# Row halves of TensorE for graph products and transposes, and Strassen's form for a dense product, in a four-layer graph network

## The chip, the cores and the metric

The kernel runs on one core of a Trainium2 chip. The metric is the device time of one execution in microseconds (us). TensorE (PE; its weight loads are listed as PEld), VectorE (DVE), ScalarE (ACT) and GpSimd (POOL) each work through their own queue in order; SyncE (SP) issues most transfers. All data is fp32.

## The reference

The input x is 128 graphs x 64 nodes x 256 features, and adj is one 64 x 64 weighted adjacency matrix that all graphs share. Each of four layers computes `x = layernorm(x + f(x))`:

```python
# layer 0: two dense products with batch norms after a graph product
A_hat = D^-1/2 (adj + I) D^-1/2
agg = einsum('nm,bmd->bnd', A_hat, x)
h   = relu(batchnorm(agg @ W1.T + b1))            # 256 -> 512
f   = batchnorm(h @ W2.T + b2)                    # 512 -> 256
# layer 1: graph product, attention over the neighbours (4 heads), an MLP
lam = eigvalsh(adj)[-1] + 1e-8
L_norm = 2 adj / lam - I
h  = relu(layernorm((L_norm x) @ Wc + bc)); x1 = h + x
o  = softmax(mask(q k^T / 8)) v @ Wo + bo         # q, k, v from x1
x2 = layernorm(x1 + o)
f  = layernorm(x2 + gelu(x2 @ W1 + b1) @ W2 + b2)
# layer 2: two graph convolutions, then LSTMs over windows of 1, 2, 3, 4 nodes
h = relu(adj (x @ Wg0 + bg0)); h = relu(adj (h @ Wg1 + bg1))
for p in 1..4: h[last node of each window of p] = lstm_p(window)
# layer 3: graph attention
Wh = x @ W; e = leaky_relu(s1_i + s2_j); f = softmax(mask(e)) Wh
```

`eigvalsh` reads the lower triangle. Means and variances of layer 0's batch norms run over all 8192 rows.

## The kernel before

**Blocks.** Rows are cut into 16 blocks of 8 graphs. A block is 512 rows, held as 4 tiles `t` of 128 rows: a tile has two graphs, graph `q` on partitions 64q to 64q+63 (`halves` names the two ranges). Node-major tiles (`tm`) have rows on the partitions; feature-major tiles (`fm`) have features there. A graph product multiplies by a 128 x 128 block-diagonal matrix with the 64 x 64 matrix in both halves: `AhT` for layer 0, `LnT` for layer 1, `bdAT` for layer 2. So half of what TensorE multiplies with there is zero. `aggregate` (line 322) does 8 such products for a block and turns node-major rows into feature-major ones on the way. `to_fm` (334) and `to_tm` (340) transpose a block with 8 TensorE transposes, and `block` has 8 more for the attention weights (764).

**Buffers.** `PS` is a stock of four PSUM tiles of 128 x 1024 fp32, each two banks wide. `mem` is a stock of SBUF tiles of the same size, eight at first. `e_ps`, a PSUM tile, is taken for the eigenvalue and given back when layer 0 ends, so layer 0's blocks work with three.

**The order** is made while the program is built. Each block is a generator that yields `step(engine, us)` before it issues that step's instructions; `flow` keeps a planned time for each engine, and lets the step go next that can start first, with stock counts, priorities of the `Stream`s and a margin. The `us` in a step is only the planner's cost. The instructions then stand in that order in each engine's queue, and semaphores keep the dependencies.

**Layer 0** (lines 387 to 601). `first_block` loads x, does the graph product with AhT, copies it (537), makes 512 features in two halves with `W1T` (346), adds b1 on ACT (549) and takes statistics on DVE (553). When all 16 are done, `bn_coeffs` makes the first batch norm's scale and shift. `second_block` applies them with relu on ACT (561), multiplies 512 features by `W2T` in 16 matmuls of 128 x 512 (566), adds b2 (575) and takes statistics (579). Then comes the second `bn_coeffs`. `eig` finds the largest eigenvalue by squaring a matrix `EIG_STEPS` = 26 times. Each round squares (468), takes the trace by a DVE product and sum and a TensorE product with ones (471 to 476), and scales the square by its reciprocal (479, 481). It is a task among the blocks, the second in the list.

**After it.** `end_block` ends layer 0 (scale and shift, transpose back, residual, layer norm). `block` is layer 1: graph product with LnT, product with Wc (358), layer norm, `to_fm`, q, k (346) and v (705), scores (730), softmax, transposes (764), attention times v (778), Wo, layer norm, `to_fm`, the MLP (346, 835), two layer norms. `gcn_block` does two graph products with bdAT and the LSTM of window 1; `unit` does longer windows, where `lstm` already uses Strassen's form (1024). `last_block` ends layer 2 and is layer 3 (two transposes, 1404, 1450, 1460). Blocks of different layers overlap, except around the batch norms of layer 0.

**Queues.** SP issues x blocks, weights and output. Layer 1's weights go into `WA` and `WB`, which layer 0 doesn't use; `wL` and the weights after it go into memory that layer 0 frees. In the program's SP queue a transfer waits for what it overwrites, and for the transfer eight before it.

Of the kernel before, what the change touches and what calls it, by code (L numbers as in the profile page):

```python
# [11 lines left out]
ALU = mybir.AluOpType  # L12
# [21 lines left out]
def kernel(ctx: ExitStack, tc: tile.TileContext, a: dict, out: bass.AP):  # L34
# [282 lines left out]

    def aggregate(ps, y, mT):

        for c in range(2):  # L320
            for t in range(NT):
                T.matmul(
                    ps[:, c, t * P : (t + 1) * P],
                    y[:, t, c * P : (c + 1) * P],
                    mT,
                    start=True,
                    stop=True,
                )

    def to_fm(ps, y):  # L330

        for c in range(2):
            for t in range(y.shape[1]):
                T.transpose(ps[:, c, t * P : (t + 1) * P], y[:, t, c * P : (c + 1) * P], ident)

    def to_tm(ps, yT):

        for t in range(ps.shape[1]):
            for c in range(2):
                T.transpose(ps[:, t, c * P : (c + 1) * P], yT[:, c, t * P : (t + 1) * P], ident)  # L340
# [46 lines left out]
    with c0:  # L387
# [9 lines left out]
        W2T = ctile([P, 4, D], "W2T", wp)  # L397

        def later_loads():
            for k in cols:  # L400
                if k != "b1":
                    yield step("Q", 1.0)
                    nc.sync.dma_start(cols[k], a[f"L0_gnn_{k}"])
            yield step("Q", 6.0)
            nc.sync.dma_start(W2T, by_chunk(a["L0_gnn_W2"]))
            yield step("V", 1.2)
            V.tensor_tensor(adj2, bdA[:, :N], bdA[:, N:], ALU.add)

            V.tensor_scalar(cap1, adj2, 0.0, BIG, ALU.is_gt, ALU.mult)
            V.tensor_scalar(cap1, cap1, -1.0e9, None, ALU.add)  # L410

            V.tensor_scalar(cap3, adj2, 0.0, 2.0, ALU.not_equal, ALU.mult)
            V.tensor_scalar(cap3, cap3, -1.0, BIG, ALU.add, ALU.mult)
# [31 lines left out]

        def eig():
# [18 lines left out]
            for _ in range(EIG_STEPS):  # L465
                yield step("T", 0.5)
                pm = pse(P)
                T.matmul(pm, M, M, start=True, stop=True)
                yield step("V", 0.6)
                t_ = etile("etmp")  # L470
                V.tensor_tensor(t_, pm, ident, ALU.mult)
                d_ = etile("ed", 2)
                V.reduce_sum(d_[:, 0:1], t_, axis=AX.X)
                yield step("T", 0.4)
                p_ = pse(2)
                T.matmul(p_[:, 0:1], ones, d_[:, 0:1], start=True, stop=True)
                yield step("V", 0.5)
                r_ = etile("er", 1)
                V.reciprocal(r_, p_[:, 0:1])
                M = etile("eM")  # L480
                V.tensor_scalar(M, pm, r_, None, ALU.mult)
# [17 lines left out]
            V.tensor_tensor(LnT, t_, ident, ALU.subtract)  # L499

# [22 lines left out]
        def first_block(i):  # L523
            if i >= len(early):
                yield step("Q", 6.0, sl=1)
                xs = mem.take()
                nc.sync.dma_start(tm(mem[xs]), x_blk[i])
            else:
                xs = early[i]
            yield step("T", 1.8, ps=1, sl=1)  # L530
            ps = PS.take()
            ag = mem.take()
            aggregate(fm(PS[ps]), tm(mem[xs]), AhT)
            mem.give(xs)
            yield step("V", 1.25, ps=-1)
            aggT = fm(mem[ag])
            V.tensor_copy(aggT, fm(PS[ps]))
            PS.give(ps)
            for hf in range(2):
                dst = fm(Xs[i]) if hf == 0 else H[i]  # L540
                yield step("T", 3.45, ps=1)
                ps = PS.take()
                mm_fm(fm(PS[ps]), W1T, aggT, 2, off=2 * hf)
                if hf:
                    mem.give(ag)
                yield step("S", 1.3, ps=-1, waits=hf == 1)
                for c in range(2):
                    f = 2 * hf + c
                    S.activation(dst[:, c, :], fm(PS[ps])[:, c, :], AF.Identity, bias=cols["b1"][:, f : f + 1])
                PS.give(ps)  # L550
                yield step("V", 1.25, waits=hf == 1)
                for c in range(2):
                    V.bn_stats(st1[:, 2 * hf + c, i, :], dst[:, c, :])
            mark("l0a", i)

        def second_block(i):
            sc1, sh1 = bn["bn1"]
            src = [(fm(Xs[i]) if f < 2 else H[i])[:, f % 2, :] for f in range(4)]
            yield step("S", 2.8)
            for f in range(4):  # L560
                S.activation(src[f], src[f], AF.Relu, scale=sc1[:, f : f + 1], bias=sh1[:, f : f + 1])
            yield step("T", 6.9, ps=1)
            ps = PS.take()
            for c in range(2):
                for f in range(4):
                    T.matmul(
                        fm(PS[ps])[:, c, :],
                        W2T[:, f, c * P : (c + 1) * P],
                        src[f],
                        start=(f == 0),  # L570
                        stop=(f == 3),
                    )
            yield step("S", 1.3, ps=-1)
            for c in range(2):
                S.activation(H[i][:, c, :], fm(PS[ps])[:, c, :], AF.Identity, bias=cols["b2"][:, c : c + 1])
            PS.give(ps)
            yield step("V", 1.25)
# [6 lines left out]
        tasks[1:1] = [(None, eig, 0)]  # L584
        tasks[4:4] = [(None, later_loads, 0)]
# [7 lines left out]
        tasks += [(lambda: ready(("bn1",)), lambda i=i: second_block(i), 0) for i in blocks]  # L593
# [7 lines left out]
        flow([Stream(6, 0, tasks)], {"T": 2.0})  # L601
        PS.give(0)
# [5 lines left out]
        for k, w in zip(("Wc", "Wq", "Wk", "Wv", "Wo", "W1", "W2"), (Wc, Wq, Wk, Wv, Wo, W1, W2)):  # L608
            nc.sync.dma_start(w, by_chunk(a[f"L1_gnn_{k}"]))
# [21 lines left out]
    def end_block(i):  # L631
# [9 lines left out]
        yield step("T", 0.9, ps=1)  # L641
        ps = PS.take()
        to_tm(tm(PS[ps]), H[i])
        mark("h", i)
        yield step("V", 1.25, ps=-1)
        V.tensor_tensor(x, tm(PS[ps]), tm(mem[xin]), ALU.add)
# [5 lines left out]
    def block(i):  # L652
        x = X[i]
        mark("begun", i)
        yield step("T", 1.8, ps=1, sl=1)
        ps = PS.take()
        s_xp = mem.take()
        aggregate(fm(PS[ps]), x, LnT)
        yield step("S", 1.05, ps=-1)
        S.copy(mem[s_xp], PS[ps])  # L660
# [14 lines left out]
        yield step("T", 0.9, ps=1, sl=1)  # L675
        ps = PS.take()
        s_x1 = mem.take()
        to_fm(fm(PS[ps]), y)
        yield step("S", 1.05, ps=-1)
        x1T = fm(mem[s_x1])  # L680
        S.copy(mem[s_x1], PS[ps])  # L681
# [44 lines left out]
        for b in range(8):  # L726
            t, s = b // 2, b % 2
            for u in range(2):
                for r in range(2):
                    T.matmul(  # L730
                        pq[s * N : (s + 1) * N, r, 2 * t + u, :],
                        qT[r * N : (r + 1) * N, u, b * N : (b + 1) * N],
                        kT[r * N : (r + 1) * N, u, b * N : (b + 1) * N],
                        start=True,
                        stop=True,
                    )
# [22 lines left out]
        yield step("T", 0.9, ps=1, sl=1)  # L759
        ps = PS.take()  # L760
        s_a = mem.take()
        pt = PS[ps].rearrange("p (g m) -> p g m", g=8)
        for g in range(8):
            T.transpose(pt[:, g, :], e[:, g, :, :].rearrange("p r m -> p (r m)"), ident)
# [3 lines left out]
        S.copy(mem[s_a], PS[ps])  # L768
        PS.give(ps)
        yield step("T", 2.0, ps=1, sl=1)  # L770
# [3 lines left out]
        for b in range(8):  # L774
            t, s = b // 2, b % 2
            for u in range(2):
                for r in range(2):
                    T.matmul(
                        po[r * N : (r + 1) * N, u, b * N : (b + 1) * N],
                        v[r * N : (r + 1) * N, b, u, :],  # L780
                        aT[r * N : (r + 1) * N, 2 * t + u, s * N : (s + 1) * N],
# [18 lines left out]
        yield step("T", 0.9, ps=1, sl=1)  # L800
        ps = PS.take()
        s_x2 = mem.take()
        to_fm(fm(PS[ps]), y)
        yield step("S", 1.4, ps=-1)
        x2T = fm(mem[s_x2])
        for c in range(2):
            S.activation(
                x2T[:, c, :], fm(PS[ps])[:, c, :], AF.Identity, scale=g2c[:, c : c + 1], bias=be2c[:, c : c + 1]
# [394 lines left out]
    def gcn_block(i):  # L1203
        yield step("T", 1.8, ps=1, sl=1)
        ps = PS.take()
        s_a = mem.take()
        aggregate(fm(PS[ps]), X[i], bdAT)
# [5 lines left out]
        S.copy(mem[s_a], PS[ps])  # L1213
# [12 lines left out]
        yield step("T", 1.8, ps=1, sl=1)  # L1226
        ps = PS.take()
        s_a = mem.take()
        aggregate(fm(PS[ps]), h1, bdAT)
        mem.give(s_h1)  # L1230
        yield step("S", 1.05, ps=-1)
        S.copy(mem[s_a], PS[ps])
# [120 lines left out]
    def last_block(i, t0=0, nt=NT):  # L1353
# [14 lines left out]
        yield step("T", 0.9 * r, ps=1)  # L1368
        ps = PS.take()
        px = tm(PS[ps])[:, :nt, :]  # L1370
        to_tm(px, hb)
# [3 lines left out]
        V.tensor_tensor(x, px, x, ALU.add)  # L1375
# [3 lines left out]
        yield step("T", 0.9 * r, ps=1, sl=1)  # L1379
        ps = PS.take()  # L1380
        s_xT = mem.take()
        px = fm(PS[ps])[:, :, : nt * P]
        to_fm(px, x)


        yield step("S", 0.3 + 1.1 * r, ps=-1)
        xT = fm(mem[s_xT])[:, :, : nt * P]
        pairs, into = (ap.rearrange("p c (u e k) -> p c u e k", e=2, k=P) for ap in (px, xT))
        S.copy(into[:, :, :, 0], pairs[:, :, :, 0])
        for h in range(2):  # L1390
            S.copy(into[:, :, :, 1, halves[1 - h]], pairs[:, :, :, 1, halves[h]])
# [244 lines left out]
```

## Time and profile before

| | |
|---|---|
| three runs | 2438.67, 2440.18, 2441.17 us; median 2440.18 |
| the profiled execution | 2439.17 us; span from first to last instruction 2437.4 us |
| mean granted TensorE clock | 0.983 |
| first product stage of layer 0 | 8 to 155 us, PE busy throughout |
| second product stage | 161 to 276.5 us, PE busy throughout |
| waits of PE for its longest single release | 6.7 us, at the start (line 440) |
| granted clock in 283 to 427 us, where layer 1 begins | 0.93 |

The profile's page gives each engine's busy time and share of the span. A row such as `L322 PE MATMUL ps<-LnT,x 128*128 128x128 f32 x16` is line, engine, operation, output and inputs (moving operand first), the rows and columns of the array in use, the moving size, and the count. One fp32 matmul of the program is two loads and two matmul records; an fp32 transpose is one of each. In a timeline the first two numbers are the start and the length in us, and equal records that follow each other are one row. In a table of stretches each engine's busy time is followed by its record count, then come granted clock, DMA share and GB/s.

### The profile page before, as it was taken

Reading aid. Unit: us, or ns where it says so; the run is one execution under the profiler, and the core shown is the slowest. Engines: PE = TensorE matmul, PEld = TensorE weight load, DVE = VectorE, ACT = ScalarE, POOL = GpSimd, SP = SyncE. Lnnn points to the kernel's source line nnn. Section 1 sums busy time; section 2 is a strip of 40 time slices with the busy share of each in tenths; the row PEclk is TensorE's granted clock in tenths of the full one; section 3 lists DMA queues with packets and bytes.
Section 4 is the critical chain, followed back from the end, with each engine's and each line's share of the span. In section 5 each row is a group of like instructions: output and inputs, shape, how many; then the busy total and the mean of one; then the engine's idle time right before and its main releaser. Section 6 shows DMA issues by size and latency. Waiting matters only on the chain. (4 is left out here: it accounts for less than half of the span.)

```text
span 2437.4 us, 33965 instructions
## 1 busy us (share of the span) xinstructions
PE 2348.3 (96%) x13700; PEld 1798.9 (74%) x13700; DVE 1215.1 (50%) x2864; ACT 1169.9 (48%) x2138; POOL 566.7 (23%) x426
## 2 busy tenths in 40 slices
PE   8999889999999999999999999999999999998997
PEld 5544567766676666676676788899999888887785
DVE  4542377646475345744462433344435444455446
ACT  2255453543444444335544444444444654468766
POOL 0000034222333222422231221222212222122112
PEclk9999989999999999999999999999999999999998
DMA  5110111000000000000010000000001000001111
GB/s 172 44 52 0 40 31 49 27 9 10 1 10 18 10 9 10 1 10 34 20 61 1 18 1 1 1 18 1 1 1 35 1 9 10 18 27 66 40 35 44
DMA packets 40974, 57.47 MB, mean 24 GB/s; under 512 B 4592, under 2 KB 33904, under 8 KB 40816
## 3 DMA queue, kind: packets, MB, share of 16 engines
q1 hardware_dynamic: 39712, 54.22, 6.9%
q8 instruction: 107, 1.75, 0.3%
q10 hardware_dynamic: 1104, 1.08, 0.1%
q14 instruction: 51, 0.42, 0.1%
HBM read 38.52 MB, written 16.78 MB: 23 GB/s over the span
## 5 line engine op out<-in xcount | busy, mean ns | idle before, releaser
L1024 PE MATMUL ps<-x,x 128*128 128x256 f32 x1024 | 248.6, 380 | 0.7 <-DVE t L1092 0.7
L1024 PEld LDWEIGHTS ps<-x,x 128*128 128x128 f32 x1024 | 191.5, 190 | 26.4 <-issue 1.6
L314 ACT ACTIVATE x<-x,ln_nm,ln_rs 128x256 f32<-128x256 f32 x196 | 103.7, 592 | 97.0 <-DVE ln_nm L311 95.5
L1024 PE MATMUL ps<-t,x 128*128 128x256 f32 x576 | 141.0, 379 | 0.0
L308 POOL TENSOR_TENSOR ln_rs<-ln_rs,neghalf 128x4 f32<-128x4 f32 (+1 forms) x72 | 70.5, 980 | 231.1 <-DVE ln_rs L274 217.3
L1024 PEld LDWEIGHTS ps<-t,x 128*128 128x128 f32 x576 | 108.6, 190 | 14.6 <-issue 0.4
L346 PE MATMUL ps<-t,W1T 128*128 128x512 f32 x256 | 115.2, 593 | 0.0
L952 PE MATMUL ps<-h,wL 128*128 128x192 f32 (+2 forms) x504 | 111.6, 375 | 0.0
L952 PEld LDWEIGHTS ps<-h,wL 128*128 128x128 f32 x504 | 79.1, 190 | 27.6 <-issue 26.7
L272 DVE BATCH_NORM_STATS2 ln_st<-x 128x6 f32<-128x256 f32 x256 | 98.2, 404 | 0.5
L1100 ACT ACTIVATE t<-t,bih 128x512 f32<-128x512 f32 (+2 forms) x63 | 41.0, 652 | 107.6 <-DVE t L1090 105.9
L952 PE MATMUL ps<-h,x 128*128 128x256 f32 x384 | 86.8, 379 | 0.0
L964 ACT ACTIVATE t<-ps,bih 128x512 f32<-128x512 f32 (+3 forms) x104 | 61.5, 642 | 44.0 <-PE ps L952 43.9
L294 POOL TENSOR_TENSOR ln_rs<-ln_rs,neghalf 128x4 f32<-128x4 f32 x32 | 36.9, 1153 | 188.8 <-DVE ln_rs L274 188.6
L346 PEld LDWEIGHTS ps<-t,W1T 128*128 128x128 f32 x256 | 46.3, 190 | 46.4 <-issue 46.4
L952 PEld LDWEIGHTS ps<-h,x 128*128 128x128 f32 x384 | 72.9, 190 | 10.3 <-issue 0.5
L1083 DVE COPY t<-ps 128x256 f32<-128x256 f32 (+2 forms) x63 | 23.7, 378 | 113.5 <-PE ps L1024 113.5
L273 DVE BATCH_NORM_AGGREGATE ln_mv<-ln_st 128x2 f32<-128x6 f32 x448 | 71.3, 167 | 0.0
L346 PE MATMUL ps<-t,wA 128*128 128x512 f32 x144 | 67.9, 617 | 2.8 <-ACT t L681 2.8
L952 PE MATMUL ps<-t,wL 128*128 128x512 f32 x144 | 64.9, 607 | 2.5 <-ACT t L1250 2.5
L1090 DVE TENSOR_TENSOR t<-ps,t 128x512 f32<-128x512 f32 (+2 forms) x63 | 38.1, 604 | 54.8 <-PE ps L1024 47.9
L1100 ACT ACTIVATE x<-x,bih 128x512 f32<-128x512 f32 (+2 forms) x57 | 36.6, 641 | 55.7 <-DVE x L1090 55.4
(692 smaller groups left out, 5688.2 us busy)
## 6 DMA issues: line engine op xcount, KB each, us to landing
t<-in_x_dram SPq DMA_DIRECT2D x26, 512.0 KB, 3.9
xd<-x SPq DMA_DIRECT2D x16, 512.0 KB, 2.6
x<-xd SPq DMA_DIRECT2D x6, 512.0 KB, 3.3
out_dram<-x SPq DMA_DIRECT2D x6, 512.0 KB, 3.0
wL<-in_L_gnn_Wih_dram SPq DMA_DIRECT2D x2, 1024.0 KB, 4.9
h<-in_x_dram SPq DMA_DIRECT2D x4, 512.0 KB, 4.2
x<-in_L_gnn_Whh_dram SPq DMA_DIRECT2D x2, 1024.0 KB, 4.9
t<-xd SPq DMA_DIRECT2D x4, 512.0 KB, 3.3
```

What stands on the lines that cost most here:

```text
L272: V.bn_stats(st[:, t, :], y[:, t, :])
L273: V.bn_aggr(mv[:, t, :], st[:, t, :])
L294: G.tensor_tensor(rs, rs, neghalf[:, :NT], ALU.pow)
L308: G.tensor_tensor(rs, rs, neghalf[:, :n], ALU.pow)
L314: S.activation(y[:, t, :], y[:, t, :], AF.Identity, scale=rs[:, t : t + 1], bias=nm[:, t : t + 1])
L346: T.matmul(ps[:, c, :], w[:, k, (off + c) * P : (off + c + 1) * P], yT[:, k, :], start=(k == 0), stop=(k == nk - 1),)
L952: T.matmul(spread(fm(PS[ps])[:, j, :n], q), WL[p][0][:, k, m], x_of(0, q)[:, k], start=(k == 0), stop=(k == 1),)
L964: S.activation(of(sl)[:, j], fm(PS[ps])[:, j, :n], AF.Tanh if g == 2 else AF.Sigmoid, bias=bias(g, c))
L1024: T.matmul(dst, WS[p][name](k, g), y[:, k], start=first and k == 0, stop=k == 1, skip_group_check=not first)
L1083: V.tensor_copy(y[:, 1, :], v[:, 0, :])
L1090: V.tensor_tensor(y[:, 0:2, :], v[:, 2:4, :], y[:, 0:2, :], ALU.add)
L1100: S.activation(of(act[g])[:, 0], of(act[g])[:, 0], f, bias=bias(g, 0))
```

## The change

1. `aggregate`, `to_fm`, `to_tm` and the attention transposes issue each 128-row product as two of 64 rows, one on each half of the array's rows, with the 64 x 64 diagonal block or half of the identity as the moving operand. The two halves' outputs go to different banks of the PSUM tile (`part`), and the copies out of PSUM put them together again (`joined`, `runs`).
2. Attention times v sends the output of row half r to column half r ^ u. The columns of Wq, Wk and Wv are loaded in another order to match, in three transfers each. The scores' loops are reordered, and `last_block`'s copies follow its transposes.
3. `second_block` does blocks 1 to 15 in Strassen's form: seven products of 256 x 256 by 256 x 256 in place of eight, in two-matmul pairs, with four sums of the weights made once (`W2S`, in `WB[:, 2:4]`) and the input and output sums on DVE, POOL and ACT. Block 0 keeps eight products, one feature chunk behind each relu.
4. `eig` is in a stream of its own with first priority; only each third round scales by the trace, and it gives its PSUM tile back when it ends.
5. The planner's costs are lower: 0.95 for 1.8 (graph product), 0.5 for 0.9 (transposes), 1.3 for 2.0 (attention times v).

```diff
+    def part(ps, s, g):
+        return ps[:, s * TB + g * N : s * TB + (g + 1) * N]
+    def joined(ps, n=2 * NT):
+        return ps.rearrange("p (s g e) -> p g s e", s=2, e=N)[:, :n]
...
     def aggregate(ps, y, mT):
         for c in range(2):
             for t in range(NT):
-                T.matmul(
-                    ps[:, c, t * P : (t + 1) * P],
-                    y[:, t, c * P : (c + 1) * P],
-                    mT,
+                for s, h in enumerate(halves):
+                    T.matmul(
+                        part(ps, s, c * NT + t),
+                        y[h, t, c * P : (c + 1) * P],
+                        mT[h, h],
...
-                T.transpose(ps[:, c, t * P : (t + 1) * P], y[:, t, c * P : (c + 1) * P], ident)
+                for s, h in enumerate(halves):
+                    T.transpose(part(ps, s, c * n + t), y[h, t, c * P : (c + 1) * P], ident[h, h])
...
+            V.tensor_tensor(W2S[0], a21, a22, ALU.add)
+            V.tensor_tensor(W2S[1], W2S[0], a11, ALU.subtract)
+            V.tensor_tensor(W2S[2], a11, a21, ALU.subtract)
+            V.tensor_tensor(W2S[3], a12, W2S[1], ALU.subtract)
...
-            for _ in range(EIG_STEPS):
+            for j in range(EIG_STEPS):
...
+                if j % 3 < 2:
+                    yield step("V", 0.35)
+                    M = etile("eM")
+                    V.tensor_copy(M, pm)
+                    continue
...
-            V.tensor_copy(aggT, fm(PS[ps]))
+            V.tensor_copy(runs(mem[ag]), joined(PS[ps]))
...
+            V.tensor_tensor(T1, x[:, :, v], x[:, :, u], ALU.subtract)
+            V.tensor_tensor(T2, h[:, :, v], T1, ALU.subtract)
+            G.tensor_tensor(T4, h[:, :, u], T2, ALU.subtract)
+            V.tensor_tensor(T3, h[:, :, v], x[:, :, v], ALU.subtract)
...
+            product(A11, x[:, :, u], p[:, 0, :], first=True)
+            product(W2S[0], T1, p[:, 3, :], first=True)
+            S.copy(y[:, 0, :], p[:, 0, :])
+            S.copy(y[:, 3, :], p[:, 3, :])
+            product(A12, h[:, :, u], p[:, 2, :])
+            product(W2S[3], h[:, :, v], p[:, 3, :])
+            product(W2S[1], T2, p[:, 0, :])
+            V.tensor_copy(y[:, 1, :], p[:, 0, :])
+            product(W2S[2], T3, p[:, 0, :])
+            V.tensor_tensor(y[:, 3, :], p[:, 0, :], y[:, 3, :], ALU.add)
+            V.tensor_tensor(y[:, 0:2, :], p[:, 2:4, :], y[:, 0:2, :], ALU.add)
+            product(A22, T4, p[:, 0, :])
...
-        flow([Stream(6, 0, tasks)], {"T": 2.0})
-        PS.give(0)
+        flow([Stream(1, 0, [(None, eig, 0)], urgent=True), Stream(6, 1, tasks)], {"T": 2.0})
...
+            if k in ("Wq", "Wk", "Wv"):
+                for m, j in ((slice(0, P), slice(0, P)), (slice(P, P + N), slice(P + N, 2 * P)), (slice(P + N, 2 * P), slice(P, P + N))):
+                    nc.sync.dma_start(w[:, :, m], src[:, :, j])
...
-                        po[r * N : (r + 1) * N, u, b * N : (b + 1) * N],
-                        v[r * N : (r + 1) * N, b, u, :],
-                        aT[r * N : (r + 1) * N, 2 * t + u, s * N : (s + 1) * N],
+                        po[halves[r ^ u], u, b * N : (b + 1) * N],
+                        v[halves[r], b, u, :],
+                        aT[halves[r], 2 * t + u, s * N : (s + 1) * N],
```

## The prediction

> **What bounds the kernel now.** I read the page's busy shares first, then the stretches of the span, then TensorE's own timeline at a fine scale.
>
> ```profile
> span 2437.4 us, 33965 instructions
> PE 2348.3 (96%) x13700; PEld 1798.9 (74%) x13700; DVE 1215.1 (50%) x2864; ACT 1169.9 (48%) x2138; POOL 566.7 (23%) x426
> ```
>
> TensorE is busy for 96% of the span and every other engine for half or less. The same by stretch (span, then busy time of PE, PEld, DVE, ACT, POOL):
>
> ```profile
> 161.00:276.50 115.50, 115.50 (x291) 53.28 (x290) 28.27 (x64) 62.81 (x94) 0.00 (x0) 0.98 0.00 0
> 283.00:427.00 144.00, 127.86 (x1005) 95.74 (x1005) 101.93 (x281) 77.70 (x113) 54.07 (x38) 0.93 0.17 51
> 427.00:1160.00 733.00, 713.25 (x4905) 497.35 (x4904) 402.49 (x902) 317.44 (x403) 217.95 (x132) 0.98 0.04 12
> 1160.00:2135.00 975.00, 971.14 (x5170) 839.67 (x5169) 431.89 (x856) 446.04 (x939) 227.06 (x163) 1.00 0.04 12
> 2135.00:2437.40 302.40, 269.36 (x1749) 224.23 (x1747) 162.56 (x570) 220.58 (x522) 63.43 (x77) 0.96 0.13 43
> ```
>
> PE's idle time is 16 us at the start of layer 1, 20 us in the rest of layers 1 and 2, 33 us at the end. Everywhere else the time is TensorE's stream, so an edit is priced by what it does to that stream. PE's busy time alone can't price it (the tail of each matmul overlaps the next); I use the distance from one row's start to the next row's start:
>
> ```profile
> 424.50 1.84 PE L905 MATMUL ps<-av,t 128*128 128x1 f32 x16
> 661.12 1.21 PE L730 MATMUL ps<-t,h 64*64 64x64 f32 x64
> 662.26 2.05 PE L322 MATMUL ps<-LnT,x 128*128 128x128 f32 x16
> 664.25 2.08 PE L778 MATMUL ps<-x,t 64*64 64x64 f32 x64
> 2184.31 1.04 PE L334 MATMUL ps<-ident,h 128*128 128x128 f32 x8
> 2185.19 1.04 PE L334 MATMUL ps<-ident,x 128*128 128x128 f32 x8
> 1996.13 0.68 PE L1450 MATMUL ps<-ident,x 64*64 64x64 f32 x16
> 1996.74 0.70 PE L1024 MATMUL ps<-x,x 128*128 128x256 f32 x2
> 1997.28 0.59 PE L1024 MATMUL ps<-h,x 128*128 128x256 f32 x2
> ```
>
> Each fp32 matmul leaves two records; a transpose leaves one. "rows*columns" is the part of the array used. Read from it:
> - A transpose costs 0.88/8 = 0.11 us. A graph product costs 1.8 to 2.0 us for 8 matmuls, 0.112 us a record.
> - L905 streams one column, and still takes 1.84 us for 16 records, 0.11 us each after the last one's tail. So **loading 128 columns of weights takes 0.11 us by itself**; a graph product, which also streams 128 columns, is already limited by its loads.
> - L730 runs 64 records on 64x64 parts in 1.14 us, L778 the same number in 2.01 us. L730 keeps all four quarters at work: its loads of both row halves and both column halves overlap. L778 uses only the two quarters on the diagonal.
> - Changing the split costs time. Two records of 256 columns take 0.43 us. Around L1450: it takes 0.61 us where its 16 records at L778's pace (2.01/64) take 0.50, and the two L1024 records after it take 0.54. With 0.1 us before its start, going in and out costs about 0.35 us, **0.17 us a change**.
>
> [...] a load record on 64 rows and 64 columns (L1450) has a median of 135 ns, on 128 rows and 64 columns (L705) 137 ns, on 128x128 (L322) 192 ns. No row here loads 64 rows by 128 columns. [...]
>
> **The change part by part.** Counts are from the two programs' instruction orders.
>
> (a) Graph products: 64 groups (16 with AhT, 16 with LnT, 32 with bdAT). 512 matmuls on 128x128 become 1024 on 64x128. Streaming halves, but each half still loads 128 columns. With both row halves loading side by side, a round of two half-records takes 0.112 us, and there are 16 rounds, as there were 16 records: 64 x 16 x (0.112 - 0.112) = **0**. Bounds: if a load of 64 rows took half, a round would take 0.058 us: -64 x 16 x 0.054 = -55 us. If the halves loaded one after the other, +64 x 16 x 0.112 = +115 us. I take 0, by L905 and the equal 64- and 128-row loads.
>
> (b) Transposes: 768 instructions, or 96 groups of 8 (16 groups where layer 0 ends, 48 in layer 1, 32 in the last blocks). A transpose's load is shorter (L334's load record: a median of 141 ns, near the 135 of a 64-column load), so its 0.109 us is streaming. That halves to about 0.058, the spacing of L1450's rounds [...]: -96 x 8 x 0.051 = **-39 us**. If its loads go one after the other: about +6.
>
> (c) Attention's product with v, 16 groups: outputs cross (r ^ u), so four quarters work: 2.01 -> about 1.05 us, **-15**. Nothing gained: 0.
>
> (d) Scores: same products reordered; L730 is at four quarters already: **0**, at most a tenth of 1.14 us either way, 2 us over 16 blocks.
>
> (e) Strassen's form, 15 of 16 blocks: before, 32 records of 512 columns, 16 matmuls, 6.87 us (four rows of 1.72). After, 14 matmuls of 256 columns, 28 x 0.2155 = 6.03 us. -15 x 0.84 = **-12.5**. What it adds elsewhere per block: DVE three differences at 0.68 (L1339), a copy at 0.42 (L1083) and sums at 0.69 + 0.41 (L1090, L1092), 3.6 us; ACT two copies at 0.37 (L1062) and one more eviction, 1.1 us; POOL one difference, 1.3 us (L983). In this stage ACT rises from 63 to about 80 us, DVE from 28 to about 72 (the eigenvalue's work leaves it), against some 100 of PE: covered, by the blocks in flight, which get four PSUM tiles in place of three. The last blocks have no cover for the chain product, sum, product: **+3**. If the hops aren't hidden, +20.
>
> (f) Eigenvalue: 18 of 26 ones-products go, about 0.25 us each: **-4.5**. The chain runs wholly inside the first product stage, where PE is always busy; between the stages (155 to 161, 277 to 283) statistics still hold PE, since the last copy, bn_stats, bn_aggr and coefficients remain. Bound: 4 us more if the urgent squarings make PE wait, as PE runs its queue in order and everything behind them waits too; 4 less if the stalls shrink.
>
> (g) Split changes: 151 in the order before, 340 after. 189 x 0.17 = **+32**. Bound: 0.1 to 0.2 each, +19 to +38.
>
> (h) Evictions through a view that alternates between two PSUM banks every 64 elements: same element count (ACT 1.01 us, DVE 1.22). L743 already writes in runs of 64 without a price (678 ns for 512, like L1242). Taken as 0; ACT and DVE have the slack; at most 5 us where they end a wait.
>
> (i) Transfers: Wq, Wk, Wv in three pieces each, six more SP issues of about 0.5 us at 12 to 25 us, where x blocks are queued between them; the fourth x block is needed only at about 35 us. The load of W2 into wB now waits for the last Strassen product, at the end of layer 0, with wL, the small weights and two x blocks behind it; wL waited until 283.56 before as well. Four x blocks are ahead of it, where six were. Taken as 0; +3 if those two are late. W2S's four DVE sums wait for W2T, issued at 10.76 and landed by 15.97, when Wo could use its semaphore; the DVE queue behind holds the first evictions: at most 2 us.
>
> Sum: 0 - 39 - 15 - 12.5 + 3 - 4.5 + 32 = **-36 us**, of which I drop 2 for the last 240 us, where PE isn't always the limit: -34. The profiled execution took 2439.17 us (span 2437.4 and 1.8 around it), 1.0 below the median 2440.18. 2439.2 - 34 = 2405 in its terms, **2406** against the median.
>
> **The rivals.**
> 1. Half loads are half as long. L905 and the pair of 135 and 137 ns speak against it, but no row has this shape. It adds -55: 2351. Together with small gains elsewhere, 2340.
> 2. The two row halves load one after the other when each is 128 columns wide. Then (a) is +115, (b) +6 in place of -39: -34 + 115 + 45 = +126, 2566. L730 speaks against it, where row halves do overlap, but with columns split as well. It decides from the round's length: with all else as summed, the change turns slower once a round in (a) takes 0.112 + 34/1024 = 0.145 us.
> 3. The PE time is saved but not kept: Strassen's hops (+20) and waits in layer 1's ramp and at the end (10), where PE idles already. 2406 + 30 = 2436, no change.
> 4. That the halves don't come about at all is excluded: the order shows 16 instructions of 128x64 for every 8 of 128x128.
>
> **How the numbers follow.** About 0.2% (5 us) is what a measurement of this kernel can tell from no change. Own forecast (2390 to 2430): 0.52. Rival 1 (2338 to 2365): 0.24. Between my forecast and rival 3, up to 2440: 0.11, of which 0.06 is within 0.2%. Rival 2: 0.08. Other losses (evictions that wait on banks, an order that fits badly): 0.05. Faster 0.81, same 0.06, slower 0.13. The range 2338 to 2440 leaves out rival 2 and the other losses; without rival 1 it would begin at 2390.
>
> **What would show it.** Right: PE rows of a graph product (16 matmuls, 32 records) still 1.8 us or more from start to start, and next to other splits 0.35 longer; 8 halved pairs of transposes about 0.5 us; attention's product about 1 us; the second product stage about 100 us in place of 115.5; no ones-product after the first barrier. Wrong: a graph product in about 1 us (rival 1) or 3.6 (rival 2), PE idle inside the second stage above 5 us (rival 3), or ACT copies above 1.1 us.

## The result: no change

The changed kernel took 2440.78 us, the median of 12 runs (2436.29 to 2446.48), against 2440.2 before: a ratio of 1.0007, 95% interval 0.9998 to 1.0016. The forecast was 2406, with a range up to 2440.0. None of the 34 us appeared. The profiled execution took 2446.48 us, the slowest of the twelve, 5.7 above the median, and the profiled execution of the kernel before is 1.0 below that kernel's median; so of any difference between the two profiles about 7 us belong to the executions and not to the kernels.

The page of the changed kernel, its span and its busy times:

```profile
span 2444.7 us, 38027 instructions
PE 2323.0 (95%) x15636; PEld 1789.4 (73%) x15636; DVE 1255.6 (51%) x2904; ACT 1185.4 (48%) x2168; POOL 591.0 (24%) x441
```

TensorE is busy 25 us less than before, and the span is 7 us longer: what it saved, it waits. Most of those 7 us belong to the two profiled executions, as said above. The stretches of the changed kernel (span, busy time of PE, PEld, DVE, ACT, POOL, then granted clock, DMA share, GB/s), cut at its own stages:

```profile
8.00:166.40 158.40, 157.86 (x842) 93.19 (x840) 77.73 (x149) 40.49 (x63) 0.56 (x1) 1.00 0.25 70
172.20:276.20 104.00, 101.25 (x436) 82.35 (x436) 69.89 (x121) 76.48 (x140) 21.59 (x15) 0.98 0.08 25
280.70:427.00 146.30, 122.63 (x1198) 87.48 (x1199) 105.58 (x275) 77.84 (x114) 52.96 (x33) 0.86 0.17 53
427.00:1160.00 733.00, 707.59 (x5871) 477.61 (x5870) 413.70 (x920) 316.78 (x406) 225.57 (x136) 0.99 0.04 15
2135.00:2444.70 309.70, 267.32 (x1925) 220.48 (x1924) 157.01 (x554) 214.46 (x496) 62.68 (x76) 0.95 0.12 38
```

The first product stage ends at 166.4 us, 11 later than before (155). The second takes 104.0 where it took 115.5. The start of layer 1 has 24 us of idle TensorE where it had 16, and a clock of 0.86 where it had 0.93. From 427 to 1160 the idle time is 25 us, before 20.

Each operation of layers 0 and 1 nevertheless costs what the prediction said. TensorE's timeline of the changed kernel:

```profile
352.57 1.95 PE L340 MATMUL ps<-LnT,x 64*128 64x64 f32 x32
354.45 1.16 PE L884 MATMUL ps<-h 64*64 64x64 f32 x64
...
434.16 2.00 PE L340 MATMUL ps<-bdAT,x 64*128 64x64 f32 x32
436.00 0.67 PE L870 MATMUL ps<-ident,t 64*128 64x64 f32 x16
436.50 0.67 PE L361 MATMUL ps<-ident,h 64*128 64x64 f32 x16
```

From start to start, a halved graph product takes 1.84 us (434.16 to 436.00), what the full one took. Eight halved transposes take 0.50 (436.00 to 436.50; 0.88 before). Attention's product is a row of 1.16 where it was 2.08.

**Where the time went.** I gave every TensorE record the distance to the next start that it has when nothing disturbs it (429 ns for 512 columns, 216 for 256, 112 for a record of a full graph product, 56 for a halved one, 109 and 29 for a full and a halved transpose). What exceeds it I put down to idle time (the record had ended before the next began), to a split change (rows or columns of the array differ in the next record), or to the rest (half clock, and the LSTM's own irregular spacing, taken as about the same in all). In this part of the span the granted clock was 0.50 for 64 us in the kernel before and for 83 in the changed one. How much of the LSTM counts as stream and how much as rest is a choice, so only the differences between the rows are read. From the first transposes of layer 0's end to TensorE's last start, in us:

| kernel | layer 0 ends | undisturbed stream | idle | split changes | rest | sum after layer 0 |
|---|---|---|---|---|---|---|
| before | 282.6 | 1872 | 78 | 18 | 178 | 2145 |
| changed | 280.8 | 1818 | 109 | 36 | 192 | 2155 |
| e2, planner's cost 1.8 | 283.4 | 1818 | 86 | 36 | 183 | 2122 |
| e1, full products too | 275.7 | 1818 | 87 | 31 | 180 | 2115 |
| c2, planner's cost 1.4 | 279.8 | 1818 | 115 | 36 | 203 | 2173 |
| f5, order of before | 285.0 | 1818 | 102 | 31 | 188 | 2139 |

The stream is 54 us shorter, as predicted (39 + 15). Idle time took 31 of it back, split changes 18, the rest 14: 63 in all, of which about 7 belong to the two profiled executions. By stretch, the idle time grew by 8 us at the start of layer 1 and by 9 at the end (the two tables of stretches), and by 8 between 427 and 1300 us.

### The profile page after: what moved, and what is told of

The parts are those of the page before. It is cut to its first block, busy times and chain, and to the rows that moved or that the text cites. A ratio compares the mean times of both kernels' runs of the same rounds, so it can differ in the third digit from the quotient of the medians.

```text
span 2444.7 us, 38027 instructions
## 1 busy us (share of the span) xinstructions
PE 2323.0 (95%) x15636; PEld 1789.4 (73%) x15636; DVE 1255.6 (51%) x2904; ACT 1185.4 (48%) x2168; POOL 591.0 (24%) x441
## 5 line engine op out<-in xcount | busy, mean ns | idle before, releaser
L1134 PE MATMUL ps<-x,x 128*128 128x256 f32 x864 | 212.9, 381 | 1.6 <-DVE x L1193 1.0
L1134 PEld LDWEIGHTS ps<-x,x 128*128 128x128 f32 x864 | 160.6, 190 | 25.2 <-issue 2.0
L1134 PE MATMUL ps<-t,x 128*128 128x256 f32 x704 | 170.0, 380 | 0.0
L1134 PEld LDWEIGHTS ps<-t,x 128*128 128x128 f32 x704 | 132.9, 190 | 18.9 <-issue 0.8
L1062 PE MATMUL ps<-h,wL 128*128 128x192 f32 (+2 forms) x456 | 90.4, 352 | 0.0
L272 DVE BATCH_NORM_STATS2 ln_st<-x 128x6 f32<-128x256 f32 x224 | 85.4, 403 | 0.4
L1062 PEld LDWEIGHTS ps<-h,wL 128*128 128x128 f32 x456 | 70.1, 190 | 16.8 <-issue 15.8
L1062 PE MATMUL ps<-t,wL 128*128 128x512 f32 x168 | 73.7, 594 | 1.3 <-ACT t L1360 0.7
L1074 ACT ACTIVATE x<-ps,bih 128x512 f32<-128x512 f32 (+3 forms) x84 | 48.9, 634 | 52.3 <-PE ps L1062 52.1
L1062 PE MATMUL ps<-x,wL 128*128 128x512 f32 x144 | 62.9, 593 | 0.0
```

Of the source, the lines that this page charges most:

```text
L272: V.bn_stats(st[:, t, :], y[:, t, :])
L1062: T.matmul(spread(fm(PS[ps])[:, j, :n], q), WL[p][0][:, k, m], x_of(0, q)[:, k], start=(k == 0), stop=(k == 1),)
L1074: S.activation(of(sl)[:, j], fm(PS[ps])[:, j, :n], AF.Tanh if g == 2 else AF.Sigmoid, bias=bias(g, c))
L1134: T.matmul(dst, WS[p][name](k, g), y[:, k], start=first and k == 0, stop=k == 1, skip_group_check=not first)
```

## The experiments

All times are medians; ratios are to the kernel before, with their 95% intervals. Theory C blames halved products (a late clock), theory I or W the waits for ACT and DVE, theories P, R and O the order in which the planner puts the steps (P: a planned cost below the true time makes a worse order; R: one near the true time makes a good order; O: each order is a draw, good or bad by chance).

**e1, e2, e3, e4: graph products put back in full, or the planner's cost alone.**

```diff
 e1: aggregate_full: one T.matmul(fm(ps)[:, c, t*P:(t+1)*P], y[:, t, c*P:(c+1)*P], mT), at all 4 places
+    V.tensor_copy(mem[ag], PS[ps]); S.copy(mem[s_xp], PS[ps]); S.copy(mem[s_a], PS[ps])
-    yield step("T", 0.95, ps=1, sl=1)
+    yield step("T", 1.8, ps=1, sl=1)
 e2: the last two lines alone        e3: as e1, in first_block alone
 e4: aggregate_full if i < 2, in first_block and block; costs as in the changed kernel
```

> The changed kernel with only its graph products put back: 64 groups of 8 products on 128 x 128, copied out of PSUM in plain order, planned at 1.8 us; transposes, attention and layer 0 stay changed. Theory C (halved products keep TensorE at half rate after every idle stretch, and add split changes): about 6 us back in the first stage, about 5 at the start of layer 1, and 59 fewer split changes at 0.13 us, 8: 2422 us. Theory I (the time that TensorE saves is lost to waits for ACT and DVE, whatever form the products have): no change, 2436 to 2445. Theory P (an order planned with a product at 0.95 us that takes 1.8 fits badly): faster by 10 to 20, but then the kernel with the planner's cost alone is as fast.

> The changed kernel with the planner's cost of a graph product put back from 0.95 to 1.8 us, nothing else: the same instructions in another order. Theory P (order planned with a wrong cost): faster by 10 to 20 us, with PE's idle time in layers 1 and 2 down by that. Theories C and I: no change beyond 5 us either way, clock at the starts as in the changed kernel.

> The changed kernel with graph products on 128 x 128 in layer 0 alone. Theory C: first product stage ends 8 to 9 us earlier (5.8 by a clock that comes up after 4 us of work as before, where the changed kernel's records stay at double spacing until 25.7 us; 20 split changes at 0.13, 2.6), total 2432 us; layer 1 as in the changed kernel, its clock 0.5 until about 300 us less 9. Theory I: the stage is shorter by the split changes at most, total 2438 to 2441.

> The changed kernel with full products in blocks 0 and 1 of layers 0 and 1 only (4 of 64 groups), the planner's costs and nearly all split changes (338 for 340) as there. Theory C, in its narrow form (only the start of a stretch matters; once at full rate the halves keep it): full rate before 15 us in place of 25.7, and about 4 us earlier in layer 1; total 2430 to 2433. Theory I, or if the rate is lost again in the halved groups that follow: no change, 2438 to 2443.

Measured: e1 2401.6 (0.984, 0.9827 to 0.9854), e2 2416.7 (0.9904, 0.989 to 0.9917), e3 2435.0 (0.9981, 0.9974 to 0.9987), e4 2437.6 (0.9991, 0.9984 to 0.9998). The surprise is e2: **one number in the planner, with the same instructions, is worth 24 us.** e1 is 15 below e2, and that is the halved products. e3's first stage ends 7.0 us earlier than the changed kernel's (158.9 for 165.9, by TensorE's last start in it), e4's 4.4. Theory C holds for the starts, but it is the smaller part: e3 is 6 us faster than the changed kernel (its planned cost of 1.8 in layer 0 changes the order too; e4's order stays), and e4, with 4 full groups of 64, only 3, where C's narrow form expected 8 to 11. Theory I as stated (the same loss in whatever form) falls.

Where the order puts a wait, the queue behind it stops too: between 378.5 and 384.2 us no PE record starts. From the changed kernel's timeline:

```profile
377.40 1.12 PE L367 MATMUL ps<-h,wA 128*128 128x512 f32 x2
384.26 5.16 PE L367 MATMUL ps<-h,wA 128*128 128x512 f32 x8 [5.74 <-DVE t L901]
...
389.26 3.60 PE L367 MATMUL ps<-h,wB 128*128 128x512 f32 x8
```

The next product waited 5.74 us for a sum on DVE. After it, eight records took 5.16 us where the next eight took 3.60: the granted clock was 0.50 from 385 to 387 us and 1.00 from 388 on, and 1.5 us more went with it. PE's waits between 300 and 1300 us (line, what it waited for, us in total, times, longest), first the changed kernel:

```profile
PE ps L367 <- ACT t L786: 9.1, 2, 5.6
PE ps L367 <- DVE t L901: 7.1, 2, 5.7
PE ps L354 <- DVE t L778: 5.0, 1, 5.0
```

and e2:

```profile
PE ps L354 <- ACT h L786: 6.2, 1, 6.2
PE ps L354 <- DVE t L778: 5.0, 1, 5.0
PE ps L367 <- ACT t L786: 2.3, 1, 2.3
```

The wait for L901 isn't among e2's, but e2 waits 6.2 us for L786 at the same place, and the eight records after it are as slow, 5.85 us:

```profile
382.48 1.12 PE L354 MATMUL ps<-ident,t 64*128 64x64 f32 x16 [6.16 <-ACT h L786]
383.53 5.85 PE L367 MATMUL ps<-h,wA 128*128 128x512 f32 x8
```

So these long waits are not the difference; they show what a wait costs. No single wait makes the 24 us. Idle time after layer 0 is 86 us in place of 109, and most of that lies between 427 and 1300 us, where layers 1 and 2 overlap and no wait is over 3.5 us: TensorE is idle there for 27 us in the changed kernel and for 9 in e2. The mean granted clock is 0.985 in e2 and 0.979 in the changed kernel (rest 183 for 192).

**c1, c2: the planner's cost, in the kernel before and at a middle value.**

```diff
 c1, kernel before:    -yield step("T", 1.8, ...)   +yield step("T", 0.95, ...)   (4 graph products)
 c2, changed kernel:   -yield step("T", 0.95, ...)  +yield step("T", 1.4, ...)
```

> The kernel before with one number changed: the planner's cost of a graph product 0.95 us in place of 1.8, while the product itself stays as it was. Theory P (a cost below the true time makes orders in which TensorE waits): slower by 10 to 24 us, 2450 to 2464, with the loss in PE's idle time of layers 1 and 2. Theory O (any other order would do it; the kernel with 1.8 was only lucky): anywhere within 15 us to either side.

> The changed kernel with the planner's cost of a graph product at 1.4 us, between its own 0.95 and the true 1.8. Theory P: between the two, 2422 to 2434. Theory O: no relation to the cost, as likely outside.

Measured: c1 2451.7 (1.0047, 1.0035 to 1.0059), as P expects, and as O allows. c2 2465.7 (1.0104, 1.0091 to 1.0117): not between 2441 and 2417 but 25 above the higher. P falls.

**c3, c4: one part alone on the kernel before.** c3 takes the new `aggregate` and its copies with the old cost; c4 the new transposes, their copies and their new costs.

> The kernel before with only its 64 graph products in row halves and the copies that follow, planned at 1.8 us as before. Theory C (rate and split changes): 110 more split changes at 0.13 us, 14; about 6 at the start and 5 at layer 1's start by the late clock: slower by 20 to 27, 2460 to 2467. Theory N (halves cost nothing but the split changes, the late start is something else): slower by 10 to 15, 2450 to 2455.

> The kernel before with only its 96 groups of transposes in row halves, their copies and their planned costs (0.5 for 0.9). Working of the prediction with the split change at the 0.13 us that the changed kernel's trace shows: 39 saved, 124 more split changes, 16: faster by 23, 2417. If waits for DVE and ACT take the place of what TensorE saves: 2430 to 2440. If halved transposes too keep the clock down at layer 1's start: 3 less saved than by the first.

Measured: c3 2465.3 (1.0105, 1.0092 to 1.0118), as C expects. Its order is that of the kernel before, so these 25 us are the halved products alone: its first stage ends 9.6 us later, the part after layer 0 is longer by 17 (split changes 11, rest 8, idle time 3 less). About 5 us of that rest are lost at one place in mid-stream (an estimate: half of the 10.2 us at half rate there). First the kernel before, then c3, which has the same steps there:

```profile
893.32 3.84 PE L322 MATMUL ps<-LnT,x 128*128 128x128 f32 x32 [1.16 <-ACT x L964]
897.00 1.95 PE L322 MATMUL ps<-bdAT,x 128*128 128x128 f32 x16
```

```profile
912.51 5.55 PE L340 MATMUL ps<-LnT,x 64*128 64x64 f32 x64 [1.01 <-ACT x L982]
917.85 3.63 PE L340 MATMUL ps<-bdAT,x 64*128 64x64 f32 x32
```

After a wait of 1.16 us the full products go on at full rate. After one of 1.01 us the halved ones begin at 56 ns a record, fall to half rate at 914.2, and the granted clock is 0.50 until 924.5. So the late clock isn't confined to the starts of layers.

c4 2448.2 (1.0032, 1.0019 to 1.0044): 8 slower where 23 faster was expected, and above 2440, the most that any theory on record allowed. Its stream is 39 us shorter as worked out; idle time after layer 0 is 100 for 78.

**f1, f5, f2: the parts in the order of the kernel before.** The order follows from the planner's costs alone, so a part with the old costs keeps it.

```diff
 f1: new to_fm, to_tm, attention transposes, their copies; every step(...) as before
 f5: f1 + po[halves[r ^ u], ...], the scores' loops, Wq/Wk/Wv in three transfers each
 f2: f5 + the new aggregate and its copies
```

> The kernel before with its 96 groups of transposes in row halves and all its planned costs kept, so that every step stands in the order of the kernel before. (With the planned costs lowered too, the same edit took 2448.2 us.) Theory O (what the halves save is lost by the new order that the lower costs lead to): 39 saved, 121 split changes at 0.13 us, 16: 2417 us, PE's idle time after layer 0 within 8 us of the kernel before. Theory W (what TensorE saves turns into waits for ACT and DVE in any order): 2432 to 2448, idle time 15 us or more above.

> The kernel before with halved transposes and attention times v on four quarters (r ^ u, with the weights' transfers), planned costs kept, so in the order of the kernel before. Theory O: f1 less 15: 2402 us. Theory W: 2425 to 2445.

> As f5, with the 64 graph products in row halves as well: all of the change but layer 0's Strassen form and eigenvalue, in the order of the kernel before. Theory O with theory C (halved products cost split changes and a late clock): 72 more split changes than f5 at 0.13 us, 9, and 11 by the clock at the two starts: 20 above f5, 2422 us. Theory W: 2440 or more.

Measured: f1 2437.2 (0.9992, 0.9985 to 0.9998), f5 2437.0 (0.999, 0.9983 to 0.9996), f2 2459.5 (1.0075, 1.0062 to 1.0088). Keeping the order doesn't save the gain: of 54 us of stream, f5 keeps 3. Theory W expected this; O's 2417 and 2402 are missed by 20 and 35. With shorter durations in the old order TensorE reaches the same waits earlier: idle time is 102 us for 78, split changes take 13, the rest 10. f2 is 22.5 above f5, as C expects. f5 shows one more loss: its first stage ends 2.3 us later than f1's, 1.5 of it at 39 us, where TensorE stands idle among the early blocks; the longer transfer queue of Wq, Wk and Wv is the only edit there.

**f3: is it the clock?**

```diff
+        warm = WB[:, 0, :TB]
+        V.memset(warm, 1.0)
+        for _ in range(3):
+            T.matmul(PS[1][:, :TB], warm[:, :P], warm, start=True, stop=True)
```

> The changed kernel with three extra products of 128 x 128 by 512 columns of ones, on TensorE's idle time before 7 us, planner and order untouched; their result is overwritten. Theory C1 (halved products can't bring the clock up, but keep it up once it is there): the halved products at the start run at 56 ns a record in place of 106, first stage 5 to 6 us shorter, total 2435. Theory C2 (the clock falls again under halved products alone): full rate at first, then half rate again before 20 us, total 2438 to 2441. Theory C3 (it is not the clock but the first transfers or the split that slows them): spacing unchanged, 2441.

Measured: 2442.3 (1.0005, 0.9996 to 1.0014). The course is C2's: full rate at first, half rate again before 20 us. f3's timeline, and below it its PE busy time, granted clock, DMA share and GB/s in stretches of it:

```profile
7.21 0.49 PE L475 MATMUL ps<-etmp,An 128*128 128x128 f32 x2 [0.67 <-DVE etmp L473]
...
8.51 6.30 PE L340 MATMUL ps<-AhT,t 64*128 64x64 f32 x64
14.74 0.79 PE L504 MATMUL ps<-eM 128*128 128x128 f32 x2
15.46 3.68 PE L340 MATMUL ps<-AhT,t 64*128 64x64 f32 x32
19.07 0.79 PE L504 MATMUL ps<-eM 128*128 128x128 f32 x2
19.66 3.58 PE L367 MATMUL ps<-t,W1T 128*128 128x512 f32 x4
23.07 0.39 PE L504 MATMUL ps<-eM 128*128 128x128 f32 x2
```

```profile
9.00:13.00 4.00, 4.00 (x46) 0.55 1.10 325
13.00:17.00 4.00, 4.00 (x34) 0.50 1.02 313
17.00:21.00 4.00, 4.00 (x26) 0.50 0.83 233
21.00:25.00 4.00, 4.00 (x9) 0.74 1.04 274
```

The squaring of `eM` serves as a clock: 0.79 us at half rate, 0.39 at full. At 7.21 us TensorE is at full rate (the same product took 0.80 in the kernel before), and its first halved records are 56 ns apart. At 9.4 the clock goes to 0.50. What took it isn't shown by f3: besides 0.9 us of halved products there were gaps of 0.67 and 0.54 us just before them. But ten us of halved products, nearly without a gap, don't bring it back (107 ns a record). After 3.4 us of 512-column products it is back. In the changed kernel itself half rate lasts until 25.4 us, through 12 us of halved products with two squarings (9.3 to 21.3, a pair each 213 ns) and 4.1 us mostly of products of 512 columns; before, with full products from 8.0 on, the full rate came at 10.9, 2.9 us after the first of them.

The same at layer 1's start, first e1, where the granted clock comes up during 4.7 us of full products (0.63 in the stretch from 285 to 289 us, 1.00 from 289 on) and a product with Wc takes 3.62:

```profile
283.99 4.71 PE L351 MATMUL ps<-LnT,x 128*128 128x128 f32 x22 [3.42 <-ACT x L314]
...
290.06 3.62 PE L386 MATMUL ps<-wA,t 128*128 128x256 f32 x16
```

and then the changed kernel, where it is still 0.50 after 7 us of halved ones, up to 301.9 us, and that product takes 6.40:

```profile
289.11 5.15 PE L340 MATMUL ps<-LnT,x 64*128 64x64 f32 x44 [3.42 <-ACT x L314]
...
296.44 6.40 PE L379 MATMUL ps<-wA,t 128*128 128x256 f32 x16
```

**g and h: a true cost, or a draw?** Costs of 1.7 and 1.9 (a product takes 1.84) in the kernel before, the changed kernel, and the changed kernel with full products.

> The changed kernel with the planner's cost of a graph product at 1.7 us. So far the same instructions took 2440.8 us (0.95), 2465.7 (1.4) and 2416.7 (1.8). Theory R (a cost near the true time gives a good order): within 6 us of 2417. Theory O (each order is a draw, whatever the cost): 2415 to 2466, with PE's idle time going with it.

> The changed kernel with the planner's cost of a graph product at 1.9 us. Theory R: within 6 us of 2417. Theory O: 2415 to 2466.

> The kernel before with the planner's cost of a graph product at 1.7 us in place of 1.8 (with 0.95 it took 2451.7). Theory R: within 6 us of 2440. Theory O: a draw from about as wide a spread as the changed kernel's, 2430 to 2470, whose middle lies above the changed kernel's by what the edits are worth.

> The kernel before with the planner's cost of a graph product at 1.9 us. Theory R: within 6 us of 2440. Theory O: 2430 to 2470.

> The changed kernel with its graph products put back to 128 x 128, planned at 1.7 us: the same order of steps as the halved form at 1.7, which took 2429.0 us. By the clock at the two starts (about 10) and 60 fewer split changes at 0.13 us (8): 2411, 18 below. If the gain of 15 at a cost of 1.8 (2401.6 for 2416.7) was a draw of the order: anywhere from 2400 to 2435.

> The same at 1.9 us, where the halved form took 2422.6 us. By the clock and the split changes: 2405. If a draw: 2400 to 2435.

All times by the planner's cost of a graph product (us):

| cost | before | changed | changed, full products | changed less before | full less halved |
|---|---|---|---|---|---|
| 0.95 | 2451.7 (c1) | 2440.8 | | -10.9 | |
| 1.4 | | 2465.7 (c2) | | | |
| 1.7 | 2446.2 (g) | 2429.0 (g) | 2412.2 (h) | -17.1 | -16.8 |
| 1.8 | 2440.2 | 2416.7 (e2) | 2401.6 (e1) | -23.5 | -15.1 |
| 1.9 | 2464.6 (g) | 2422.6 (g) | 2406.6 (h) | -42.0 | -16.0 |

Theory R falls too, for the kernel before: a cost 0.1 off the old one moves it by 6 or 24 us, though none of its instructions changes; and the changed kernel at 1.7 is 12 above e2. (Its three costs near the true time do beat the two lower ones, but five orders can't tell that from chance.) Each cost gives another order, and orders of the same instructions lie up to 49 us apart. The edits are worth 11 to 42 us at equal cost, 23 in the mean of the four pairs. Halved products cost 15 to 17 in each of the three pairs, which have the same order of steps; in the order of the kernel before it was 25 (c3) and 22.5 (f2 less f5). And the kernel before stood in the best of its four orders, the changed kernel in the fourth of its five.

## Why the prediction was wrong

**The step that failed: the sum took the order and the waits as given.** It priced each edit by TensorE's stream ("Everywhere else the time is TensorE's stream") and left PE's idle time as it stood, but for 30 us in rival 3. The stream came out as worked out. The idle time did not stay: it took 31 us of the 54 back. How much it takes depends on the order: 8 us in e2's, and 24 in the order of the kernel before, where f5 kept only 3 of the 54. That a shorter stream meets its waits earlier is the reading that fits these figures; no run varied the waits alone.

The change's own fifth point, the planner's costs, wasn't priced at all, though an order made with 0.95 for a step of 1.84 can be another order throughout. "An order that fits badly" had a share in 0.05. Put back to 1.8, that number gives 24 us. With it, and with full products, the kernel takes 2401.6, near the 2406 of the forecast, but not for its reasons alone: at costs of 1.7 and 1.9 the same kernel takes 2412.2 and 2406.6.

The difference of 0.6 us splits like this: everything but halved products and planner's cost -38.6 (e1 less before; -34.0 and -58.0 at costs of 1.7 and 1.9), halved products +15.1 (e2 less e1), cost 0.95 for 1.8 +24.0 (changed less e2). In another order the same parts have other sizes, as the table shows.

Point by point:

- The idle time that it started from: its lines give 24 us in the rest of layers 1 and 2, 4 of them after 1160 us, not 20.
- (a) Graph products, taken as 0. Right at full clock: 1.84 us, so rivals 1 and 2 (1.0 and 3.6) are both out. The load records of 64 rows by 128 columns have a median of 188 ns (L340), where those of 128x128 have 192 in the kernel before (L322). Wrong in the sum: 15 to 17 us in the new order, 22.5 to 25 in the old. In the three pairs of the new order about 9 us of that are split changes (4 to 6 after layer 0, 4 to 4.5 in it), which stood under (g). The remainder is in what the table calls rest: at a cost of 1.8 the halved form has 5 us more of it in layer 0, and 3 after it. At layer 0's start half rate lasts until 25.4 us in the changed kernel and until 10.9 in the kernel before; what it costs after layer 0 wasn't measured apart. The prediction had no term for a rate that differs with the form of the product.
- (b), (c) Transposes and attention: right, -39 and -15 in the stream. (d) Scores: a row of 1.16 us for 1.21 before (e1 and the changed kernel), right.
- (e), (f) Layer 0. The stream there is 16 us shorter (e1), as worked out. But its idle time is 6 us longer: PE waits 2.5 us inside the second stage, near the 3 of (e), and 2.4 in the first for a squaring, within (f)'s bound of 4; and the squarings are no longer there to be done while the batch norm is waited for. What the table calls rest adds 3. So e1's layer 0 is 7 us shorter from its first product on (269.1 for 275.9), not 14.
- (g) Split changes: too dear at 0.17. After layer 0 there are 146 more with no idle time at them, and they took 18 us more, 0.12 each. 189 would be 23, not 32.
- (h) Copies that join the halves: right. L765 takes 1.012 us, as L660 did; L574 1.225 for 1.224.
- (i) Transfers, taken as 0 with a bound of 3: 2.3 in f5, by the first stage; the changed kernel has no such gap, with 0.5 us of idle time in the whole stage.
- Rival 3 (saved but not kept) had the outcome right, 2436 for 2440.8, with sizes that were not: Strassen's hops took 3 us and not 20, the waits at layer 1's start and at the end 17 and not 10 (24 for 16 and 42 for 33 by the stretches). The order and the clock were not in it. So its nearness is luck in part.

## What to carry to other kernels

Where a planner writes the order, a change of durations is two changes: the work, and a new draw of the order. Try the edit with several neighbouring costs, and the old kernel too, before its worth is read; here one pair could say anything from -48 (e2 and the kernel before at 1.9) to +26 (c2 and the kernel before). Look at the clock after every idle stretch, a wait of 1 us in mid-stream included (1.01 us in c3, then 0.50 from 914.2 to 924.5): halved products like these are better kept from places where TensorE is at half rate, since 12 us of them left it there in the changed kernel. Full products in the first blocks alone (e4) bought 3 us here, little more than the noise; full products throughout, 15 to 17. A kernel of these parts that beats both is e1: halved transposes, crossed attention outputs, Strassen's form and full graph products, 2401.6 us (0.984).

## What the runs showed of the hardware

Halved graph products, issued in pairs on the two row halves, ran at half rate for as long as nothing but them and a few squarings ran: 12 us in the changed kernel (9.3 to 21.3) and 10 in f3, 107 ns a record in both. In c3 they lost a full rate that was there, 1.7 us after a wait of 1.01 us, where full products kept it after 1.16. Without a wait they held it, in a stretch of 128 halved records with one squaring among them (130.65 to 138.50), of which this is the end:

```profile
133.00 5.58 PE L340 MATMUL ps<-AhT,t 64*128 64x64 f32 x96
```

That is 58 ns a record in the changed kernel, at a granted clock of 1.00. Whether the half rate goes with the 64 rows or with the 64 streamed columns wasn't tried, nor how long a full rate would last, nor how short a wait is enough to lose it. The clock column reads 1.00 at the start of both kernels, where the spacing shows half rate: 213 ns a record for full products up to 10.9 us in the kernel before (112 after it), 107 for halved ones in the changed kernel. The trace's first clock record stands at 10.9 us in the one and at 25.4 in the other, so the 1.00 of the changed kernel's first stretch above hides its slow start.
